# Attention over gathered neighbours: the transposes of later keys placed between the scores of the next duo and the values of the present one

## The chip, the cores and the metric

The kernel runs on one core of a Trainium2 chip. The metric is the device time of one execution in microseconds (us). The time before is the median of three runs; a measured difference of less than about 0.3% cannot be told from none.

## The reference

One layer of a graph network: a masked attention with eight heads over 4096 nodes, then a mixture of eight experts of which each node uses two.

```python
x = x + _L0_gnn_ref(_layernorm(x), adj, Wks, Wqs, Wvs, Wo)
x = x + _L0_ffn_ref(_layernorm(x)[None], Wg, bg, W1, b1, W2, b2)[0]

def _L0_gnn_ref(node_matrix, adjacency_matrix, Wks, Wqs, Wvs, Wo):
    adj = jnp.maximum(adjacency_matrix, eye)
    q, k, v = (einsum('nd,hdk->hnk', node_matrix, W) for W in (Wqs, Wks, Wvs))
    scores = einsum('hqk,hmk->hqm', q, k) * kd ** (-0.5)
    scores = scores + 0.01 * eye - 1e16 * (1.0 - adj)
    att = softmax(scores, axis=-1)
    return einsum('hqm,hmk,hko->qo', att, v, Wo)
```

N is 4096, the model width 512, the key width 64. The adjacency matrix is sparse, and its first rows and columns are denser than the last ones. In the expert part (`_L0_ffn_ref`), a gate of 8 columns picks two experts for each node, and their outputs are summed with softmax weights.

## The kernel before, in words

The program has four stages in one instruction stream. It is scheduled by hand (`tc.manual_schedule()`, L106): each engine runs its instructions in the order in which the Python code issues them. Engines are TensorE (PE), VectorE (DVE), ScalarE (ACT), GpSimd (POOL) and the DMA issuer SP.

1. Up to about 455 us: layer norm, projections to q, k and v, and lists of the neighbours that occur in each tile of 128 queries. Keys, values and mask words go to `kv_d` in DRAM, queries to `q_d`.
2. Up to about 1640 us: attention, the stage of the change.
3. A short stretch that works out which rows go to which expert (L1142 to L1198).
4. From about 1692 us: the experts.

In stage 2 each of the 32 query tiles is a list of steps (L644 to L655). A step treats 128 keys, or twice 128 keys for the two halves of the queries. There are three kinds: "own" (the tile's own rows), "both" (128 gathered keys for all 128 queries), and "split" (two gathers of 128 keys, each for 64 queries). `ROOM` (L31) says how many steps of each kind a tile has. All in all there are 32 own, 115 both and 123 split steps. Steps of one tile are taken two at a time, in the order of the list; such a pair, or a single last step, is a duo (L659 to L662). There are S = 144 duos.

A step passes through four functions:

- `gather` (L686): an indirect DMA on POOL's queue for each 128 keys (own rows come by SP) into a row of a ring of 24 rows (`RING`, L630). `issue` (L1070) asks for duos up to five ahead (`AHEAD`, L1062), as far as rows of the ring are free.
- `turn` (L716): PE transposes the keys, four transposes for 128 keys, into PSUM tile `pkT` (L723). ACT copies `pkT` to `kT` in SBUF (L725). DVE unpacks the mask bits to `t` (L735), and for own steps makes `m` (L742).
- `scores` (L749): PE multiplies `kT` by the queries into `ps` (L760): for a split step 64 matmuls on 64x64 pieces of the array, for the others 16 on 64x128 pieces. ACT takes the exponential into `pr` (L767). DVE applies the mask (L771 or L773).
- `values` (L779): PE multiplies `pr` by the values in the ring into the tile's accumulator `o` (L788), 32 matmuls on 128x64 pieces for a step.

Behind the last duo of a tile, `end_of` (L803) divides by the sums at once (`scale`) and puts jobs into later iterations: `flip_o` (transposes, L820) one later, `project` (L828) and `residual` (L837) two later. After every fourth tile, `route` (L855) puts in jobs that spread over some eight iterations: `norm` on ACT (L890), `flip` (transposes, L901), `gate` (L910), `rank` and `place` on DVE (L919 to L942), `number_places` (PE, tile `pp`, L947) with `keep_places` (DVE, L954), `pick` and `weigh` (DVE, then one exponential on ACT, L1011), `finish`, and `scatter` (POOL, L1029).

The order around the change is that of the main loop (L1117 to L1138). In iteration n it issues: scores of duo n+1, values of duo n, the loads of `issue`, the jobs of iteration n, and then the turn of duo n+3. Three duos are turned ahead of the loop (L1112 to L1115).

PSUM is a second order that matters. `ps_r` (L635) has three tiles of two banks each, and `bank` (L666) hands them out in rotation to everything in this stage but the accumulator `o`: `ps` and `pkT`, one tile for each step, and the tile of each PE job (`po`, `py`, `px`, `pl`, `pp`). So the tile handed out as number k is the buffer of number k-3, and a PE group that takes it must wait until ACT or DVE has emptied that one. The accumulator `o` has one buffer of two banks. In SBUF, `kT` and `pr` have four buffers, `t` six.

Of the kernel before, what the change touches and what calls it, by code (L numbers as in the profile page):

```python
# [70 lines left out]
def fast(tc, dram, flag, x, adj, Wks, Wqs, Wvs, Wo, Wg, bg, W1, b1, W2, b2, out):  # L71
    with ExitStack() as ctx:
        _fast(ctx, tc, dram, flag, x, adj, Wks, Wqs, Wvs, Wo, Wg, bg, W1, b1, W2, b2, out)


def _fast(ctx, tc, dram, flag, x, adj, Wks, Wqs, Wvs, Wo, Wg, bg, W1, b1, W2, b2, out):
# [248 lines left out]
    with ExitStack() as s1:  # L325
# [198 lines left out]
        def job(n, f, *args):  # L524
            jobs.setdefault(n, []).append(lambda: f(*args))
# [108 lines left out]
    with ExitStack() as s2:  # L634
# [76 lines left out]
        def load_xi(i):  # L711
            xs_[i] = mid.tile([P, W], F32, tag="x", bufs=10, name=f"x_{i}")
            queue = nc.sync if i < NT - 3 else nc.scalar
            queue.dma_start(out=xs_[i][:, :D], in_=x[ts(i, P), :])
# [355 lines left out]
        def issue(upto, n):  # L1070
            nonlocal issued, rows_
            while issued < min(upto, S):
                sts = [steps[s] for s in duos[issued]]
                need = sum(max(1, len(st["at"])) for st in sts)
                if any(behind[(rows_ + k) % RING] > n for k in range(need)):
                    return
                for s in duos[issued]:
                    st = steps[s]
                    if st["k"] == 0:
                        load_q(st["i"])  # L1080
                    st["to"] = []
                    for x in range(max(1, len(st["at"]))):
                        k = rows_ % RING
                        behind[k] = issued
                        rows_ += 1
                        st["to"].append(ring[:, k * KVW : (k + 1) * KVW])
                        gather(s, x)
                issued += 1
# [3 lines left out]
        def load_weights(n):  # L1092

            for k in range(PARTS):
                over_ = range(k * SW // KVW, min(RING, ((k + 1) * SW - 1) // KVW + 1))
                if issued == S and wparts[k] is None and all(behind[r] <= n for r in over_):
                    load_part(k, ring[:, k * SW : (k + 1) * SW].bitcast(F32))

        def load_part(k, t):
            v = t.rearrange("p (e f) -> p e f", e=E)  # L1100
            from_, c = (W1, k) if k < DC else (W2, k - DC)
            for e in range(E):
                nc.sync.dma_start(out=v[:, e], in_=from_[e, ts(c, P), :])
            wparts[k] = v

        def duo(f, n):
            if n < S:
                for s in duos[n]:
                    f(s)
# [6 lines left out]
        n = 0  # L1116
        while n < S or any(k >= n for k in later):  # L1117
            duo(scores, n + 1)
            duo(values, n)
            if n < S:  # L1120
                end = steps[duos[n][-1]]
                if end["last"]:
                    end_of(end["i"], n)
                    load_xi(end["i"])
                issue(n + 1 + AHEAD, n)
                load_weights(n)
            todo = later.pop(n, [])
            if n >= S:
                todo.sort(key=lambda job: -job[0])
            for _, job in todo:  # L1130
                job()
            duo(turn, n + 3)
            if n == S:
                s3.close()
                wff = ctx.enter_context(tc.tile_pool(name="wff", bufs=1))
                for k in range(PARTS, DC + HC):
                    load_part(k, wff.tile([P, SW], F32, name=f"w_{k}"))
            n += 1  # L1138
# [854 lines left out]
```

## Time and profile before

| What | Value |
|---|---|
| Median of 3 runs | 2074.48 us (2071.14 to 2076.76) |
| The profiled execution | 2230.39 us, its span 2228.6 us |
| PE busy in the span | 2003.9 us (90%), 25491 matmuls |
| DVE, ACT, POOL busy | 959.3, 790.9, 611.7 us |
| Attention stage (455 to 1640 us): PE busy | 1021.4 of 1185.0 us, at a granted clock of 0.93 |
| The same: DVE, ACT, POOL busy; DMA share | 534.8, 527.0, 464.9 us; 0.71 |
| Expert stage (1692 to 2228.6 us): PE busy | 517.7 of 536.6 us |

The profile is of one execution on the chip. A line of a group names a line of the kernel, the engine, the operation, the tile written and those read, the pieces of the array in use (64*64 means 64 rows by 64 columns of it), the shapes and a count; then busy time and mean duration, and the idle time of the engine ahead of these instructions with its causes. "issue" as a cause means that the engine waited for nothing that the profile shows. In a timeline, each line is a run of like instructions: start, duration from the first start to the last end, engine, line. Matmuls are pipelined, so that the end of one may lie after the start of the next. A wait for several semaphores is put down to the one that came last.

### The profile page before, as it was taken

Reading aid. Unit: us, or ns where it says so; the run is one execution under the profiler, and the core shown is the slowest. Engines: PE = TensorE matmul, PEld = TensorE weight load, DVE = VectorE, ACT = ScalarE, POOL = GpSimd, SP = SyncE. Lnnn points to the kernel's source line nnn. Section 1 sums busy time; section 2 is a strip of 40 time slices with the busy share of each in tenths; the row PEclk is TensorE's granted clock in tenths of the full one; section 3 lists DMA queues with packets and bytes.
Section 4 is the critical chain, followed back from the end, with each engine's and each line's share of the span. In section 5 each row is a group of like instructions: output and inputs, shape, how many; then the busy total and the mean of one; then the engine's idle time right before and its main releaser. Section 6 shows DMA issues by size and latency. Waiting matters only on the chain. (4 is left out here: it accounts for less than half of the span.)

```text
span 2228.6 us, 59742 instructions
## 1 busy us (share of the span) xinstructions
PE 2003.9 (90%) x25491; PEld 1329.7 (60%) x25491; DVE 959.3 (43%) x2501; ACT 790.9 (35%) x1152; POOL 611.7 (27%) x721
## 2 busy tenths in 40 slices
PE   9899999979999879888969697887967999999996
PEld 4344444459887757767858586776754444444443
DVE  3455655525444434534535344443554333333332
ACT  3232333235554534534535253443421222222221
POOL 2000000054444345433243443324122222222221
PEclk9999999989999979989989798998978999999998
DMA  9778775287777568767576575766686455565542
GB/s 371 253 251 257 255 246 179 77 350 252 246 259 257 201 228 266 249 206 239 190 267 232 202 255 204 255 201 222 227 278 195 104 115 113 111 144 111 110 72 44
DMA packets 193411, 462.01 MB, mean 207 GB/s; under 512 B 30384, under 2 KB 46768, under 8 KB 193008
## 3 DMA queue, kind: packets, MB, share of 16 engines
q0 software_dynamic: 67024, 249.44, 36.8%
q1 hardware_dynamic: 101808, 177.51, 24.8%
q10 hardware_dynamic: 24304, 31.11, 4.0%
q8 instruction: 206, 3.38, 0.6%
q14 instruction: 69, 0.57, 0.1%
HBM read 385.37 MB, written 72.64 MB: 206 GB/s over the span
## 5 line engine op out<-in xcount | busy, mean ns | idle before, releaser
L696 POOL DMA_INDIRECT ring<-kv_d,idx x361 | 407.3, 1128 | 978.1 <-ACT l L303 438.0
L760 PE MATMUL ps<-q,kT 64*64 64x64 f32 (+1 forms) x10224 | 356.5, 242 | 112.4 <-issue 96.0
L773 DVE SCALAR_TENSOR_TENSOR pr<-t,pr 128x1024 f32<-128x1024 uint16 x238 | 284.9, 1226 | 369.8 <-ACT pr L767 367.4
L760 PEld LDWEIGHTS ps<-q,kT 64*64 64x64 f32 (+1 forms) x10224 | 304.3, 151 | 166.1 <-issue 135.9
L788 PE MATMUL o<-ring,pr 128*64 128x65 f32 x8640 | 308.9, 228 | 31.6 <-issue 31.3
L725 ACT COPY kT<-pkT 128x512 f32<-128x512 f32 (+1 forms) x270 | 198.8, 783 | 375.5 <-PE pkT L723 268.6
L767 ACT ACTIVATE pr<-ps 128x1024 f32<-128x1024 f32 x270 | 271.4, 1025 | 139.4 <-PE ps L760 104.0
L788 PEld LDWEIGHTS o<-ring,pr 128*64 128x64 f32 x8640 | 282.1, 141 | 52.3 <-issue 37.5
L1341 PE MATMUL ph<-ring,xT 128*128 (+1 forms) x528 | 238.2, 594 | 0.8 <-ACT xT L1303 0.8
L723 PE MATMUL pkT<-ident,ring 128*128 128x128 f32 x1572 | 211.3, 282 | 18.3 <-issue 16.7
L723 PEld LDWEIGHTS pkT<-ident,ring 128*128 128x128 f32 x1572 | 180.0, 145 | 46.3 <-issue 38.7
L1392 POOL DMA_INDIRECT out_dram<-y,r x66 | 101.8, 1542 | 366.2 <-ACT y L1387 266.8
L1370 PE MATMUL py_e<-ring,hT 128*128 (+1 forms) x396 | 182.3, 596 | 1.6 <-ACT hT L1363 1.6
L1341 PEld LDWEIGHTS ph<-ring,xT 128*128 128x128 f32 (+1 forms) x528 | 91.3, 183 | 99.8 <-issue 98.7
L1387 ACT ACTIVATE y<-y,wt 128x512 f32<-128x512 f32 x66 | 47.6, 722 | 269.6 <-DVE y L1383 229.8
L604 PE MATMUL pv<-wv,xT 128*128 128x512 f32 x256 | 131.3, 608 | 0.0
L604 PE MATMUL pk<-wk,xT 128*128 128x512 f32 x256 | 130.4, 621 | 0.7 <-ACT xT L399 0.7
L589 PE MATMUL pq<-xT,wq 128*128 128x512 f32 x256 | 125.9, 607 | 0.0
L1029 POOL DMA_INDIRECT xs_d<-x,slot_i x64 | 64.6, 1010 | 203.2 <-DVE t L735 90.2
L828 PE MATMUL py<-wo,oT 128*128 128x512 f32 x256 | 119.3, 609 | 0.7 <-ACT oT L822 0.7
L1346 DVE COPY h<-ph 128x512 f32<-128x512 f32 x66 | 45.6, 692 | 169.6 <-PE ph L1341 166.1
L1370 PEld LDWEIGHTS py_e<-ring,hT 128*128 128x128 f32 (+1 forms) x396 | 67.2, 183 | 76.0 <-issue 74.1
(293 smaller groups left out, 1893.7 us busy)
## 6 DMA issues: line engine op xcount, KB each, us to landing
adj<-in_adj_dram SPq DMA_DIRECT2D x64, 1024.0 KB
wo<-in_L_ffn_W_dram SPq DMA_DIRECT2D x72, 256.0 KB
kv_d<-kvr ACTq DMA_DIRECT2D x32, 516.0 KB
ring<-kv_d SPq DMA_DIRECT2D x32, 516.0 KB
r<-xs_d SPq DMA_DIRECT2D x57, 258.0 KB
ring<-in_L_ffn_W_dram SPq DMA_DIRECT2D x56, 256.0 KB
xt<-in_x_dram SPq DMA_DIRECT2D x32, 256.0 KB
q_d<-qT ACTq DMA_DIRECT2D x32, 256.0 KB
```

Source lines behind the costliest of these rows:

```text
L589: nc.tensor.matmul(pq, w["q"][:, c, ts(p, P)], xTs[b][:, c, :], start=(c == 0), stop=(c == DC - 1),)
L604: nc.tensor.matmul(pk, xTs[b][:, c, ts(t, P)], w[n][:, c, :], start=(c == 0), stop=(c == DC - 1),)
L696: nc.gpsimd.indirect_dma_start(out=g, out_offset=None, in_=kv_d, in_offset=bass.IndirectOffsetOnAxis(ap=idx[i // GL][:, i % GL, a : a + 1] ...
L723: nc.tensor.transpose(pk[:, x * NP + p, :], g[:, ts(p, P)], ident)
L725: nc.scalar.copy(kT[:, : nk * NP], pk[:, : nk * NP])
L760: nc.tensor.matmul(ps[c : c + nk, r, p * P + x * nq : p * P + (x + 1) * nq], kT[r * KD : (r + 1) * KD, p, c : c + nk], q[r * KD : (r + 1) ...
L767: nc.scalar.activation(pr.rearrange("p h q -> p (h q)"), ps.rearrange("p r f -> p (r f)"), AF.Exp)
L773: nc.vector.scalar_tensor_tensor(pr, st["t"].unsqueeze(1).to_broadcast([P, H, P]), 0.0, pr, op0=ALU.is_gt, op1=ALU.mult,)
L788: nc.tensor.matmul(o[c * HALF : (c + 1) * HALF, h // NP, (h % NP) * VW : (h % NP + 1) * VW], pr[:, hd * NP + p, c * HALF : (c + 1) * HALF] ...
L828: nc.tensor.matmul(hold["py"], hold["oT"][:, c, :], wo[:, c, :], start=(c == 0), stop=(c == NP - 1),)
L1341: nc.tensor.matmul(ph[a], xTs[b][:, c, a], w, start=(c == 0), stop=(c == DC - 1), skip_group_check=b >= FULL,)
L1370: nc.tensor.matmul(py[a], hTs[b][:, c, a], w, start=(c == 0), stop=(c == HC - 1), skip_group_check=b >= FULL,)
```

## The change

One line moves. The turn of duo n+3 is issued directly behind the scores of duo n+1 and ahead of the values of duo n, and no longer at the end of the iteration behind the values, the loads and the jobs. The prologue, the count of instructions, the buffers and the loads are the same. For the last three duos there is nothing left to turn, so that 141 turns move.

```diff
         while n < S or any(k >= n for k in later):
             duo(scores, n + 1)
+            duo(turn, n + 3)
             duo(values, n)
             if n < S:
                 end = steps[duos[n][-1]]
...
             for _, job in todo:
                 job()
-            duo(turn, n + 3)
             if n == S:
                 s3.close()
```

`duo(f, n)` (L1106) calls f for each step of duo n. `turn` issues transposes on PE (L723), the copy on ACT (L725) and the mask's unpacking on DVE (L735, L742); it issues no DMA. On each of the three engines these instructions come ahead of the values' matmuls, the division of a tile's end and the jobs, where they came behind them.

## Prediction

> **What bounds the kernel now.** I read the page's busy times, then the table of stages, the waits of PE within the attention, and last the timeline around them.
>
> ```profile
> PE 2003.9 (90%) x25491; PEld 1329.7 (60%) x25491; DVE 959.3 (43%) x2501; ACT 790.9 (35%) x1152; POOL 611.7 (27%) x721
> ...
> PE ps L760 <- issue: 91.1, 123, 9.5
> PE o L788 <- issue: 28.2, 38, 2.9
> PE pkT L723 <- issue: 9.0, 13, 3.0
> PE ps L760 <- DVE place L954: 7.1, 5, 1.8
> ...
> PE ps L760 <- ACT oT L822: 2.9, 5, 1.8
> PE ps L760 <- ACT kT L725: 1.5, 3, 1.0
> PE pkT L723 <- ACT x2T L903: 1.2, 2, 0.9
> ```
>
> PE is busy for 90% of the span, the next engine for 43%. So the sum of PE's work sets the time, and this change adds no matmul. The waits (600 to 1640 us; total, times, longest) say what PE lacks in the attention: 128 us "issue", mostly in the middle of a run of matmuls, where no data can be late, and only 7.1 + 2.9 + 1.5 + 1.2 = 12.7 us for results of other engines. Those 12.7 us are all that a better order can win from other engines. A third cost is in the timeline of PE (start, duration, line, count):
>
> ```profile
> 562.01 0.66 PE L820 MATMUL po<-ident,on 128*128 128x128 f32 x4
> 562.51 1.47 PE L723 MATMUL pkT<-ident,ring 128*128 128x128 f32 x12
> 563.91 2.58 PE L760 MATMUL ps<-q,kT 64*64 64x64 f32 x80
> 566.42 2.09 PE L788 MATMUL o<-ring,pr 128*64 128x65 f32 x64
> 568.44 3.70 PE L828 MATMUL py<-wo,oT 128*128 128x512 f32 x8
> 571.98 1.47 PE L723 MATMUL pkT<-ident,ring 128*128 128x128 f32 x12
> ```
>
> Subtract each start from the end of the line above. A job (L820, L828) and a turn (L723), both on 128*128 pieces, overlap by 0.16 us (562.67 less 562.51; 572.14 less 571.98). Turn to scores, scores to values, values to job overlap by 0.07 us only. So whenever the piece of the array changes, 0.09 us of overlap is lost. And a turn of 12 behind a job takes 1.47 us, behind values 1.53 us:
>
> ```profile
> 1106.35 2.09 PE L788 MATMUL o<-ring,pr 128*64 128x65 f32 x64
> 1108.37 1.53 PE L723 MATMUL pkT<-ident,ring 128*128 128x128 f32 x12
> ```
>
> **What the Trainium skill says.** "TensorEngine Tiling (Array Packing)", section Key Properties: changing the tiling mode, not just the tile, drains the TensorE. The trace agrees, and prices it: 0.09 us of overlap, and 0.06 us for a slower first transpose. "TensorE: Matmul & The Clock Gate", section on the array's architecture: ScalarE and VectorE are strict FIFOs, and only weight loads are pulled ahead on PE. The trace agrees: `keep_places` (L954, below) runs only after the masks queued ahead of it. "Runtime: NRT & Kernel Launch", section Instruction fetch mechanics: instructions come by DMA in blocks of 256. The trace has 206 packets and 3.38 MB on such a queue, 16 KB each; that this is what "issue" in mid-run waits for, no run here shows.
>
> **The change, part by part.** Call the PE groups S (scores), T (turn), V (values), J (jobs). The order S V J T becomes S T V J.
>
> *Changes of the piece.* Without PE jobs a round is S V T before and S T V after: three changes in both, each with 0.07 us of overlap whichever pair it is, so nothing. With PE jobs J and T were neighbours on the same pieces: S V JT had three changes, S T V J has four. I went through the loop's job times (L848 to L860, L1040 to L1060) for each of the 141 iterations that turn something: 30 hold `flip_o`, 30 `project`, 12 more only flips, gates or `number_places`. That is 72 x (0.09 + 0.06) = +10.8 us, all on PE, beside nothing.
>
> *Waits that go.* The five for `place` look like this one:
>
> ```profile
> 1224.25 0.19 PE L947 MATMUL pp<-chosen,below 128*128 128x32 bf16 x1
> 1224.69 2.35 DVE L773 SCALAR_TENSOR_TENSOR pr<-t,pr 128x1024 f32<-128x1024 uint16 x2
> 1224.78 1.04 PE L723 MATMUL pkT<-ident,ring 128*128 128x128 f32 x8
> 1226.96 0.18 DVE L954 TENSOR_TENSOR place<-pp,start_e 128x32 f32<-128x32 f32 x1
> 1227.20 0.29 PE L760 MATMUL ps<-q,kT 64*64 64x64 f32 x4 [1.38 <-DVE place L954]
> ```
>
> `pp` is done at 1224.4, DVE empties it only behind two masks, at 1227.1, and the first score behind the turn needs that PSUM buffer. After the change the scores of one duo and, where `pp` is the iteration's only bank, that whole pair (2 us) pass before the buffer comes round: tile k waits for tile k-3, so behind S1 S2 T1 T2 J the next first turn waits for J. Two of the five are of this kind and vanish. Three have `pp` and `po` together; there the second score waits for `pp`. Its need comes 1.0 us later and DVE arrives 0.5 us later (the turn's unpacking, 0.56 us for three, L735, is now ahead of it), so 1.4 becomes about 0.45 us on my reckoning at each. Total 7.1 becomes 1.4: -5.7 us. The oT waits follow `weigh`, whose exponential holds ACT until DVE has done `pick` (2.2 us); the buffer's next user is again a turn, 2 us of scores later, but DVE starts 0.9 us later. 2.9 becomes 0.8: -2.1 us. The kT waits (second score behind the copy of the first turn) and the x2T waits go: -2.7 us.
>
> *Waits that come.* The second turn of a pair now takes the buffer of the first score, so it waits for that exponential in every iteration. Bounds from this place:
>
> ```profile
> 1215.51 2.06 PE L760 MATMUL ps<-q,kT 64*128 64x128 f32 x32
> 1216.72 1.95 ACT L767 ACTIVATE pr<-ps 128x1024 f32<-128x1024 f32 x2
> 1217.50 1.15 PE L788 MATMUL o<-ring,pr 128*64 128x65 f32 x32
> ```
>
> The first exponential (mean 1.025 us) ends at 1217.74. In the new order T1 would start at 1217.50 in place of V, and T2 after 4 transposes (0.11 each, plus 0.06) at 1218.0, after 8 at 1218.45. Margin 0.2 to 0.7 us if ACT is free when the score ends, and it is: its four operations of a duo (two of 1.0, two of 0.5 to 1.0) fit into S, T and V of 5 to 6 us. With jobs it is late in five iterations where two copies and two `norm`s (0.75 each) queue up: about 0.5 us each, +2.5 us. From below it cannot be a gain; from above see the first rival.
>
> *What is moved past what.* `turn` issues no DMA, so SP's and POOL's queues keep their order. Gathers wait for V of an earlier duo, which now comes one T later in its round, while T comes earlier by V and J, at most about 8 us in all. The gathers run far ahead: the last starts at 1584.7 and the last transpose at 1622.6, and the landing of the software queue's packets, 5.5 us in the middle and 7.0 at the ninth tenth from issue, leaves 25 us or more behind the first 15 duos and 14 us at the fourth, the first that moves. If that cover were gone, PE would stand for what is missing. On DVE, `scale` and the jobs now stand behind the unpacking (0.3 to 0.85 us); they need V, which ends one T later anyway. V waits for `pr` of the round before, and has T more time.
>
> *Sum.* 10.8 - 5.7 - 2.1 - 2.7 + 2.5 = +2.8 us. Against the profiled execution 2230.4 becomes 2233.2. The median of the timed runs is 155.9 us less, about the 128 us of "issue" with its slowed clock; that part is likely smaller there. The sum consists of PE time at full clock and of queues behind ACT and DVE, so I add it as it is: 2074.5 + 2.8 = 2077.3, within the 0.3% (6.2 us) that a measurement of this kernel tells from no change. The case's own range, from half the savings kept to all of them, is 2072 to 2083.
>
> **The rivals.** *The exponential in the way (slower).* The margin of T2 is 0.2 us at its smallest. If ACT starts the first exponential later than in the quoted place, each turn pays; it decides from 0.25 us of lateness on. At a mean of 0.1 us in 141 iterations that is +14: 2091. For it: the same buffer serves every round, and own and both steps have the small margin. Against it: 0.06 us from the end of the score to ACT's start in the quoted place. Half of it gives 2084.
> *Smoother supply (faster).* 91.1 + 28.2 us are lost in the middle of S and V, the runs dense in instructions. T and J between them spread the dense runs. If a tenth goes, -12: 2065. Against it: S and V were neighbours before, and V and S are so in half of the new rounds; and the timed runs have less of this idle time.
> *Turning was never the limit.* If the waits stay and the drains too, 2085; if the drains hide in the starved stretches and nothing else moves, 2074.
> *Keys late.* With 25 us of lead, 2% at most.
>
> **How the numbers follow.** The forecast 0.45 (a quarter of it above 2081), exponential or kept waits 0.30, smoother supply 0.20, others 0.05. Faster by over 0.3%: 0.21; within: 0.38; slower: 0.41. The range reaches into both rivals: 2066 to 2089.
>
> **What would show it.** Right: PE's L723 lines of 8 or 12 at about the 1.53 us form in every round; L788 to a job and a job to L760 with 0.07 us of overlap; the wait for `place` at 2 us or less; PE's busy time up by some 5 to 11 us. Wrong: a wait of L723 for `pr` L767 of over 5 us in total (the first rival); "issue" at L760 and L788 well below 119 us, with a faster median (the second); any wait of L723 for DMA.

## The result, and the profile after

The changed kernel takes 2064.1 us (median of 6 runs, 2060.94 to 2068.36); the kernel before, run beside it, 2075.11 us (6 runs, 2071.14 to 2076.76). The ratio is 0.9955, 95% interval 0.9939 to 0.9971: faster by 6.0 to 12.7 us, where the forecast was +2.8 us. The profiled execution took 2068.36 us, its span is 2066.5 us.

One thing is needed to read the numbers below: whole executions of the kernel before take either about 2075 us, as in this comparison, or about 2222 us, as in its profile and in all the experiments, so the two traces differ by more than the change, and the kernel before has no trace at 2075 us.

From the page of the changed kernel: the engines' busy time, and the granted clock in 40 slices.

```profile
PE 1942.0 (94%) x25491; PEld 1283.8 (62%) x25491; DVE 959.3 (46%) x2501; ACT 785.1 (38%) x1152; POOL 571.1 (28%) x721
...
PEclk9999999999999999999999999999979999999998
```

The count of matmuls is the same, and PE is even more clearly the bound. What PE waited for in the changed kernel, 600 to 1480 us, since its attention ends some 158 us earlier than in the trace of before (total, times, longest):

```profile
PE o L788 <- issue: 22.6, 20, 2.6
PE ps L760 <- issue: 19.1, 16, 3.7
PE pkT L723 <- DMA ring<-kv_d: 6.0, 2, 5.6
PE o L788 <- DVE t L735: 2.6, 1, 2.6
PE ps L760 <- ACT x2T L903: 0.9, 3, 0.3
PE ps L760 <- DVE place L954: 0.8, 2, 0.4
PE py L828 <- issue: 0.6, 1, 0.6
PE pkT L723 <- ACT oT L822: 0.5, 1, 0.5
```

The waits for `place`, `oT` and `kT` are down to 0.8, 0.5 and nothing. There is no wait of a turn (L723) for an exponential (`pr`, L767). "issue" is 42 us where it was 128 (in 600 to 1640 us), but that difference belongs to the two executions: in a later one of the changed kernel (2291 us, below) it is 104 us. New is a wait for keys, 6.0 us. The 2.6 us at the values are put down to DVE's unpacking, which had ended 1 us before; they are of the kind of the "issue" gaps (see the table of two kinds of gap). The timeline of PE in the changed kernel (start, duration, line, count):

```profile
759.28 2.06 PE L760 MATMUL ps<-q,kT 64*128 64x128 f32 x32
761.27 1.53 PE L723 MATMUL pkT<-ident,ring 128*128 128x128 f32 x12
762.73 2.09 PE L788 MATMUL o<-ring,pr 128*64 128x65 f32 x64
764.75 2.25 PE L760 MATMUL ps<-q,kT 64*64 64x64 f32 x80
766.93 1.97 PE L723 MATMUL pkT<-ident,ring 128*128 128x128 f32 x16
768.83 2.09 PE L788 MATMUL o<-ring,pr 128*64 128x65 f32 x64
770.85 0.66 PE L820 MATMUL po<-ident,on 128*128 128x128 f32 x4
771.43 0.75 PE L760 MATMUL ps<-q,kT 64*64 64x64 f32 x36
```

The order is S T V, then J where there is one, and the overlap is 0.07 us at most of the changes (759.28 + 2.06 less 761.27; 768.83 + 2.09 less 770.85): the job is now among values and scores, with a change of piece on both sides, as the prediction had it. The turn of 12 takes 1.53 us, as priced. Everything outside the attention takes what it took: the experts 529 us in both traces, the work ahead of the attention 465 to 467 us. From the first transpose to the last value matmul it is 1177.8 us in the trace of before and 1021.6 us here.

### The profile page after: what moved, and what is told of

Its sections match the earlier page's. It is cut to its first block, busy times and chain, and to the rows that moved or that the text cites. A ratio compares the mean times of both kernels' runs of the same rounds, so it can differ in the third digit from the quotient of the medians.

```text
span 2066.5 us, 59701 instructions
## 1 busy us (share of the span) xinstructions
PE 1942.0 (94%) x25491; PEld 1283.8 (62%) x25491; DVE 959.3 (46%) x2501; ACT 785.1 (38%) x1152; POOL 571.1 (28%) x721
## 5 line engine op out<-in xcount | busy, mean ns | idle before, releaser
L696 POOL DMA_INDIRECT ring<-kv_d,idx x361 | 360.9, 1000 | 873.7 <-ACT l L303 437.1
L767 ACT ACTIVATE pr<-ps 128x1024 f32<-128x1024 f32 x270 | 270.4, 1025 | 376.1 <-PE ps L760 373.9
L760 PE MATMUL ps<-q,kT 64*64 64x64 f32 (+1 forms) x10224 | 308.5, 237 | 26.4 <-issue 24.4
L788 PE MATMUL o<-ring,pr 128*64 128x65 f32 x8640 | 297.3, 226 | 26.9 <-issue 24.0
L760 PEld LDWEIGHTS ps<-q,kT 64*64 64x64 f32 (+1 forms) x10224 | 274.8, 149 | 69.5 <-issue 56.4
L788 PEld LDWEIGHTS o<-ring,pr 128*64 128x64 f32 x8640 | 273.9, 140 | 54.6 <-issue 49.4
L723 PE MATMUL pkT<-ident,ring 128*128 128x128 f32 x1572 | 206.0, 280 | 12.7 <-DMA ring<-kv_d 6.0
L725 ACT COPY kT<-pkT 128x512 f32<-128x512 f32 (+1 forms) x270 | 198.5, 787 | 15.0 <-DMA q_d<-qT 6.7
L723 PEld LDWEIGHTS pkT<-ident,ring 128*128 128x128 f32 x1572 | 171.0, 142 | 29.8 <-issue 7.7
L1029 POOL DMA_INDIRECT xs_d<-x,slot_i x64 | 70.2, 1097 | 186.6 <-DVE x L1025 159.3
L1370 PEld LDWEIGHTS py_e<-ring,hT 128*128 128x128 f32 (+1 forms) x396 | 67.2, 183 | 75.9 <-issue 74.1
```

What stands on the lines that cost most here:

```text
L696: nc.gpsimd.indirect_dma_start(out=g, out_offset=None, in_=kv_d, in_offset=bass.IndirectOffsetOnAxis(ap=idx[i // GL][:, i % GL, a : a + 1] ...
L723: nc.tensor.transpose(pk[:, x * NP + p, :], g[:, ts(p, P)], ident)
L725: nc.scalar.copy(kT[:, : nk * NP], pk[:, : nk * NP])
L760: nc.tensor.matmul(ps[c : c + nk, r, p * P + x * nq : p * P + (x + 1) * nq], kT[r * KD : (r + 1) * KD, p, c : c + nk], q[r * KD : (r + 1) ...
L767: nc.scalar.activation(pr.rearrange("p h q -> p (h q)"), ps.rearrange("p r f -> p (r f)"), AF.Exp)
L788: nc.tensor.matmul(o[c * HALF : (c + 1) * HALF, h // NP, (h % NP) * VW : (h % NP + 1) * VW], pr[:, hd * NP + p, c * HALF : (c + 1) * HALF] ...
```

## The experiments

Two theories. **Supply**: PE lacks instructions in its densest runs, the scores (on the 64*64 pieces a weight load and a matmul every 14.8 ns; values take 30 ns for such a pair, transposes 109 ns), and the order and the gathers' traffic decide how much; the waits and drains of the prediction cancel. **Waits and drains**: the time is what these terms make it, and the supply is the same in every order. Ratios are to the kernel before on the same chip, with 95% intervals; code is shown as an edit of the kernel before where nothing else is said, with cuts marked by dots.

**Unchanged kernel, again.** No edit.

> The kernel before, unchanged, for a second profile. Both theories: 2071 to 2077 us. Theory 'waits' (the gain of the change is the buffer waits of scores for place, oT and kT that fall away, less four changes of the array's piece in place of three): the attention shows 15 to 25 us of PE waits for DVE and ACT, and about as much issue idle in the middle of L760 and L788 as the changed kernel has (50 us). Theory 'supply' (the gain is a smoother supply of instructions): issue idle in the middle of L760 and L788 is 12 us or more above the changed kernel's 50 us, and the waits for DVE and ACT are 10 us or less.

Measured: 2218.41 us, ratio 0.9987 (0.9968 to 1.0006), before 2221.85. The kernel does not differ from itself, as it must be, but the 2071 to 2077 us that both theories had expected were missed.

**Turn directly behind the values (S V T J).**

```diff
             duo(values, n)
+            duo(turn, n + 3)
...
-            duo(turn, n + 3)
```

> Order scores, values, turn, jobs: the turn is ahead of the jobs but still behind the values. PSUM buffers go round as in the changed kernel, but turn and jobs are neighbours on the same piece of the array, so that a round has three changes of piece again. Theory 'waits': the same waits fall away as in the changed kernel and 72 x 0.15 = 10.8 us of drains are not added: ratio to before 0.990 (2054 us), 0.986 to 0.993. Theory 'supply': scores and values are neighbours again in every round as before, so the gain is lost: ratio 0.998 to 1.001 (2071 to 2077 us).

Measured: 2215.87 us, 0.997 (0.9956 to 0.9984), before 2221.85: between the two forecasts. A second time:

> Scores, values, turn, jobs once more, beside the changed kernel. Theory 'waits': 10 us below the changed kernel. Theory 'supply': above it, ratio to before 0.997 as in the first such run.

Measured: 2210.66 us, 0.9955 (0.9938 to 0.9972), before 2220.82. Jobs and turn stay neighbours, so no drain is added; it gains 0.3 to 0.45%. The second forecast failed in both theories, as the changed kernel, run beside it, was 82 us slower.

**Turn and jobs both ahead of the values (S T J V).** The jobs' block moves with the turn.

```diff
             duo(scores, n + 1)
+            duo(turn, n + 3)
+            todo = later.pop(n, [])
...
+            for _, job in todo:
+                job()
             duo(values, n)
```

> Order scores, turn, jobs, values: the turn is where the change puts it, but the jobs come ahead of the values. PSUM buffers go round as in the changed kernel; turn and jobs are neighbours on the same piece, three changes a round. Theory 'waits': ratio 0.990 (2054 us), as without the extra drains. Theory 'supply': turn still parts scores from values, but values and the next scores are always neighbours: ratio 0.995 to 1.000 (2064 to 2075 us), not below the changed kernel's 2064.

Measured: 2403.76 us, 1.0826 (1.0796 to 1.0857): 182 us slower with the same matmuls, and far outside both forecasts (0.990, and 0.995 to 1.000). The largest wait in the whole trace of this kernel:

```profile
PE ps L760 <- issue: 135.1, 319, 1.7
```

The scores stand directly behind the values in every round and stop in mid-run 319 times. In the 104 such rounds that I compared, from 600 us on and away from the stretches in which DMAs of POOL scatter rows, the scores take 157 us more than their matmuls' own 14.8 or 57.5 ns each.

**The changed kernel on these chips.** No further edit.

> The changed kernel, unchanged, beside the kernel before on one chip. Theory 'waits' (buffer waits for place, oT and kT fall away, 10.8 us of drains come): the same 8 to 11 us less wherever it runs, ratio 0.995 to 0.997, and the waits of PE for DVE and ACT fall by some 20 us. Theory 'supply' (PE starves less in the middle of scores and values): the gain grows with the idle time that PE has there: 9 us where the kernel before takes 2075 us, 15 us or more where it takes 2222 us (ratio 0.993 or less).

Measured: 2292.41 us, 1.0324 (1.0291 to 1.0357), before 2220.82. **The sign turns over**: 71.6 us slower here, 9 us faster in the comparison of the result; both theories had expected a gain. So beside it one execution of the kernel before:

> The kernel before, for a profile from the same chip as the changed kernel. Theory 'waits': waits of PE for DVE and ACT in the attention 20 us above the changed kernel's. Theory 'supply': the issue idle in the middle of L760 and L788 is 15 us or more above it, the waits for DVE and ACT by 13 us at most.

Measured: 2226.15 us. The attention takes 1176.9 us in it and 1238.5 us in the changed kernel; all else is alike. In the timeline of the changed kernel of this job:

```profile
690.51 2.09 PE L788 MATMUL o<-ring,pr 128*64 128x65 f32 x64
692.53 0.50 PE L760 MATMUL ps<-q,kT 64*64 64x64 f32 x17
693.24 0.33 PE L760 MATMUL ps<-q,kT 64*64 64x64 f32 x4 [0.21 <-issue]
693.98 0.36 PE L760 MATMUL ps<-q,kT 64*64 64x64 f32 x5 [0.41 <-issue]
694.70 0.66 PE L760 MATMUL ps<-q,kT 64*64 64x64 f32 x26 [0.36 <-issue]
695.60 0.36 PE L760 MATMUL ps<-q,kT 64*64 64x64 f32 x6 [0.25 <-issue]
```

The 64 values take the 2.09 us that they take elsewhere; the scores behind them stop after 17 matmuls and then again and again, which is no wait for data, as one copy brought the keys of the whole step. The waits of the same kernel, 600 to 1480 us:

```profile
PE ps L760 <- issue: 78.4, 166, 2.3
PE o L788 <- issue: 14.1, 16, 1.8
PE pkT L723 <- issue: 11.6, 17, 1.8
PE pkT L723 <- ACT pr L767: 8.6, 9, 2.8
PE ps L760 <- DVE place L954: 0.8, 2, 0.4
```

And of the kernel before, in the execution of 2226 us, same stretch:

```profile
PE ps L760 <- issue: 83.2, 116, 9.6
PE o L788 <- issue: 16.1, 22, 2.9
PE pkT L723 <- issue: 8.4, 12, 2.7
PE ps L760 <- DVE place L954: 5.7, 4, 1.8
```

`place` goes from 5.7 to 0.8 as foretold, and the first rival's wait (a turn for an exponential) exists here with 8.6 us: too small for 70. The "issue" lines are hardly different (so neither forecast for this pair came true), because the gaps between single matmuls that are too short to be listed count as busy time. So I took, for each run of scores, the time from its first to its last start, less its count by the nominal distance (14.8 or 57.5 ns). By what stands ahead of it, from 600 us on, without the stretches with scatters:

| Kernel | ahead of the scores | rounds | mean excess, us | sum, us |
|---|---|---|---|---|
| before (2226) | turn | 108 | 0.48 | 51.5 |
| changed (2291) | values | 44 | 1.58 | 69.6 |
| changed (2291) | jobs | 66 | 0.52 | 34.1 |
| S V T J (2215) | turn | 44 | 0.79 | 34.8 |
| S V T J (2215) | jobs | 65 | 0.23 | 15.1 |
| S T J V (2384) | values | 104 | 1.51 | 157.2 |
| changed (2068) | values | 33 | 0.16 | - |

Scores behind transposes or jobs lose 0.2 to 0.8 us, behind values 1.5 us. In the execution of 2068 us they lose 0.16 behind values. From the first transpose to the last value matmul the scores take 49 us more in the changed kernel (2291) than in the kernel before (2226), the turns 15 more, the jobs 5 more and the values 8 less.

**Turn and scores alternating (S1 T1 S2 T2 V).**

```diff
-            duo(scores, n + 1)
+            for k in range(2):
+                for f, m in ((scores, n + 1), (turn, n + 3)):
+                    for s in (duos[m] if m < S else [])[k : k + 1]:
+                        f(s)
...
-            duo(turn, n + 3)
```

> Score, turn, score, turn, values: the finest mixture of scores and turns. Two more changes of piece in each round that has two steps on both sides (about 118 of 144), at about 0.29 us for the pair with its slower first transpose: +34 us on PE. Theory 'waits': slower than the changed kernel by that, ratio to before 1.011 (1.008 to 1.015). Theory 'supply': the dense scores are parted once more, so that a part or all of it comes back: ratio 0.990 to 1.003.

Measured: 2262.47 us, 1.0205 (1.0169 to 1.0241): 30 us below the changed kernel, although it has two more changes of piece in a round. By waits and drains alone it had to be slower. Both ranges were missed, though: they had been set for a changed kernel near 1.00, not 1.0324.

**One step's turn on each side of the values (S T1 V T2 J).**

```diff
             duo(scores, n + 1)
+            for s in (duos[n + 3] if n + 3 < S else [])[:1]:
+                turn(s)
             duo(values, n)
+            for s in (duos[n + 3] if n + 3 < S else [])[1:]:
+                turn(s)
...
-            duo(turn, n + 3)
```

> From the changed kernel: the first step's turn stays between scores and values, the second step's goes behind the values, ahead of the jobs. No dense run (scores, values) stands directly behind another. Theory 'supply, by what stands ahead' (scores that start directly behind values starve for instructions: in the profile of e4 1.58 us a round too long, 0.52 behind jobs; in that of e5 0.48 behind turns): where the kernel before takes 2222 us, about 60 us come back from e4's 2292 and about 10 go for one more change of piece in the rounds without PE jobs: 2225 to 2245, ratio 1.002 to 1.010. Where it takes 2075 us, scores behind values lose only 0.16 us in the changed kernel's profile, so nothing comes back: 2064 to 2075. Theory 'waits and drains alone': 10 us slower than the changed kernel at either place (ratio 1.037 or 1.000).

Measured: 2234.97 us, 1.0069 (1.0049 to 1.009), before 2220.12. As foretold by the supply theory. In rounds without PE jobs it has a drain more than the changed kernel, and it is 57 us below it: half a turn between values and scores is most of the cure.

**Useless transposes in the gap.** The changed kernel, with eight transposes of the identity (44 us of PE in all, by estimate) between values and scores in the 37 rounds without any job.

```diff
+            if not todo and n + 3 < S:
+                idle = bank(f"idle_{n}", [8, P])
+                for k in range(8):
+                    nc.tensor.transpose(idle[:, k, :], ident, ident)
```

> From the changed kernel: in the 37 rounds without any job, eight transposes of the identity (useless work) stand between values and the next scores: 8 x 0.11 us and one more entry and exit of their piece of the array, 0.3 us, so 37 x 1.2 = 44 us more of PE work. Theory 'supply, by what stands ahead': where the kernel before takes 2222 us they cost about nothing, since scores behind sparse work lose 1.06 us less a round: ratio 1.025 to 1.037 beside 1.032 of e4; where it takes 2075 us they cost 35 to 44 us: ratio 1.013 to 1.017. Theory 'waits and drains alone': +44 us at either place (1.052 or 1.017).

Measured: 2298.8 us, 1.0344 (1.0317 to 1.037), where the changed kernel had 1.0324 (1.0291 to 1.0357): the added PE work costs nothing that can be told from 0. In the two traces the added transposes take 38 us; the scores take 17 us less in return and the turns 11 less. So much of the time was there to be filled, though most of the cost of scores behind values stays.

**Without the gathers.** Once the 24 rows of the ring are filled, no more rows are gathered; each tile's own rows are loaded whole in their place. The attention so works on stale keys and the routing differs (the experts take 556 us); the instructions of PE are the same.

```diff
-                    out=g[:, :HV], in_=kv_d[1 + i * P : 1 + (i + 1) * P, :HV]
+                    out=g, in_=kv_d[1 + i * P : 1 + (i + 1) * P, :]
...
-                nc.gpsimd.indirect_dma_start(
...
+                if rows_ <= RING:
+                    nc.gpsimd.indirect_dma_start(
```

Order before, changed order, S V T J:

> The kernel before with the gathers left out once each of the 24 ring rows has been filled; later steps use old keys and masks, and own rows are loaded whole (580 KB in place of 516). PE, ACT and DVE do the same work. If the traffic of the gathers is what slows PE's supply of instructions: issue idle in the middle of scores and values falls from 120 us to 40 us or less and the time to 2070 to 2120 us (the 26 us stretches at the scatters may stay). If it isn't: 2200 to 2225 us.

> The changed kernel with the same gathers left out; to be compared with e10. If supply stays slow: 2270 us or more, 1.03 times e10, as with gathers. If supply is free, theory 'waits are larger than the first profile showed' (buffer waits of PE above 20 us where it isn't held up otherwise, drains 10.8 us): 9 to 12 us below e10. Theory of the prediction's sum (waits of 12.7 us): e10 plus 0 to 5 us.

> Scores, values, turn, jobs, with the same gathers left out. If supply is free and the waits are what is gained: 10 us below e11, as it has no extra drains. If only the place of turn between scores and values gains: as e10.

Measured: 2083.17, 2082.98 and 2083.0 us, each 0.9375 (at most 0.9353 to 0.9396), before 2222.32. The attention is 1005.2, 1002.9 and 1006.4 us, where it was 1177 with the gathers. The changed order is neither 70 us slower nor the 9 to 12 us faster that one theory had expected. Waits with the order before, 600 to 1480 us (lines one higher than in the kernel):

```profile
PE ps L761 <- issue: 17.1, 26, 1.5
PE o L789 <- issue: 11.1, 24, 1.1
PE ps L761 <- DVE place L955: 4.4, 4, 1.4
...
PE ps L761 <- ACT oT L823: 3.7, 6, 1.9
PE ps L761 <- ACT kT L726: 2.2, 3, 1.3
```

With the changed order:

```profile
PE ps L761 <- issue: 24.3, 41, 1.2
PE o L789 <- issue: 7.5, 12, 1.1
...
PE ps L761 <- ACT x2T L904: 0.9, 3, 0.3
PE ps L761 <- DVE place L955: 0.8, 2, 0.4
PE pkT L724 <- ACT pr L768: 0.8, 3, 0.3
```

4.4 + 3.7 + 2.2 = 10.3 us of waits become 2.5: -7.8 us, and -8.4 us (12.6 to 4.2) with the smaller ones for other engines. The drains, by the busy time of PE in 455 to 1640 us (first number behind the length; order before, then changed order):

```profile
455.00:1640.00 1185.00, 1107.40 (x21710) 904.83 (x21709) 594.88 (x1517) 557.90 (x697) 116.86 (x202) 0.96 0.30 96
```

```profile
455.00:1640.00 1185.00, 1116.82 (x21718) 903.02 (x21717) 598.82 (x1522) 554.68 (x699) 120.58 (x203) 0.96 0.30 97
```

+9.4 us, but some 2 us of it are work of the experts, which start 2.1 us earlier. From the first transpose to the last value matmul the same 21166 matmuls keep PE busy for 953.4 and 960.5 us: +7.1 us. -8.4 and +7.1 leave -1.3 us; the attention is 2.3 us shorter and the times differ by -0.2, each from runs that spread over 6 us. For S V T J I had expected -10, as it has no added drain; that fell. Its waits do not go away:

```profile
PE ps L761 <- DVE place L955: 4.5, 4, 1.4
PE ps L761 <- ACT kT L726: 2.1, 8, 0.3
```

The PSUM tiles go round as in the changed order; what differs is that no values stand between a turn and the next scores. That this is why the waits stay was not tested.

**Every second gather.** The condition becomes the following, else as above; again stale keys.

```diff
+                if rows_ <= RING or rows_ % 2:
```

> The kernel before with about half of the gathers left out after the ring's first filling (every second row keeps its old content; own rows loaded whole). Theory 'supply under gather traffic': between 2083 and 2222 us, about 2085 to 2120, with an issue idle of 30 to 60 us in the middle of scores and values. If it doesn't come from traffic but from the gathers' mere presence: near 2200.

> The changed kernel with the same half of the gathers left out; to be compared with e13. Theory 'the sign goes with the loss to supply': at this light load 3 to 10 us below e13 (ratio 0.995 to 0.999), as beside 2075 us. If scores behind values starve at any load: 5 to 40 us above e13.

> Scores, values, turn, jobs with the same half of the gathers left out. It was 0.996 of before with all gathers and 1.000 with none, so 0.996 to 1.000 of e13 by either theory; if turn between scores and values is what gains at a light load, e14 lies below it.

Measured: 2115.74 us, 0.9492 (0.9467 to 0.9518); 2140.29 us, 0.9609 (0.9579 to 0.9638); 2116.41 us, 0.949 (0.9463 to 0.9517); before 2231.81. I had hoped that a lighter load would turn the sign to that of the comparison of the result. It does not: the changed order is 24.6 us slower, and S V T J is at the level of the order before (0.7 us more). What the scores lack, order before and changed order in turn (600 to 1480 us):

```profile
PE ps L761 <- issue: 43.0, 71, 2.8
PE o L789 <- issue: 17.6, 25, 2.5
```

```profile
PE ps L761 <- issue: 52.0, 117, 1.7
PE o L789 <- issue: 7.6, 12, 1.2
```

So the price of the changed order is 0, about 25 and about 70 us with no, half and all gathers. The wait of the scores grows and that of the values shrinks: the shortage moves to the run that now stands behind another dense one. With the gathers the traffic went, and also POOL's work on them and their writes into SBUF; these were not parted.

**Two kinds of gap in mid-run.** The "issue" gaps of over 0.15 us within a run of like matmuls are of two kinds. In the execution of 2068 us all 44 are *long*: they last 0.2 to 3.7 us, each ends at instruction 193 or 194 of a block of 256, counted over PE's instructions in the trace, and 1.2 to 1.6 us after a packet on PE's instruction queue has landed (206 packets of 16 KB bring its some 52000 instructions, so about 256 each). For example, the 64 values of this round stop once:

```profile
755.42 1.21 PE L788 MATMUL o<-ring,pr 128*64 128x65 f32 x33
758.20 1.15 PE L788 MATMUL o<-ring,pr 128*64 128x65 f32 x31 [1.57 <-issue]
```

In every other trace most gaps are *short*: their median is 0.4 us, they often follow each other at 0.72 us or twice that, and they come at any place of a block and with no fixed distance to a packet, as in the lines at 693 to 696 us above. Counts and sums in the attention:

| Order (execution, us) | long | sum, us | short | sum, us |
|---|---|---|---|---|
| before (2226) | 18 | 22.4 | 173 | 105.5 |
| changed (2291) | 8 | 8.9 | 250 | 121.2 |
| S V T J (2215) | 15 | 18.2 | 185 | 103.7 |
| S T J V (2384) | 6 | 7.8 | 355 | 157.3 |
| S T1 V T2 J (2232) | 8 | 10.3 | 222 | 112.0 |
| before, half of the gathers | 16 | 16.5 | 107 | 63.4 |
| changed, half | 5 | 6.2 | 147 | 67.2 |
| S V T J, half | 18 | 18.0 | 107 | 56.6 |
| before, no gathers | 8 | 5.2 | 56 | 28.2 |
| changed, no gathers | 3 | 1.9 | 54 | 36.5 |
| S V T J, no gathers | 6 | 4.8 | 59 | 34.2 |
| changed (2068) | 44 | 49.0 | 0 | 0 |

The change makes the long gaps fewer in all three pairs, by 13.5, 10.3 and 3.3 us, as does every order with a turn between scores and values; and it makes the short ones longer in sum, by 15.7, 3.8 and 8.3 us. The execution of 2068 us has only the kind that the change makes fewer.

Taking out the scatters alone was not tried, since a later stage uses what they write as indices.

## Why the prediction was wrong, step by step

*Changes of the piece (+10.8 us).* Right in kind, somewhat too large: 0.07 us of overlap at the new changes, and PE's busy time in the attention up by 7.1 us without gathers.

*Waits that go (-5.7, -2.1, -2.7).* Right in total: 7.8 to 8.4 us go net without gathers, 8.0 were foretold with the +2.5 below. In the execution of 2068 us `place` is left with 0.8 (1.4 foretold), `oT` with 0.5 (0.8), `kT` with none; `x2T` stays with 0.9, which I had at zero.

*Waits that come (+2.5).* Too large: none in the execution of 2068 us, 0.8 us for the turns without gathers. The first rival (each turn late for the exponential, +14) did not come; in the execution of 2291 us it shows 8.6 us.

*What is moved past what.* "25 us or more" of lead for the keys, and so 2% for "Keys late", was read from an execution whose PE stood still more often. In the execution of 2068 us PE is faster and the lead, from the landing of a gather's packets to the first transpose of its duo, shrinks to 2.3 us at its smallest behind the first 15 duos. For rows that are not gathered it fails once by 5.6 us (and once by 0.4). The changed kernel's timeline:

```profile
1281.44 2.12 PE L760 MATMUL ps<-q,kT 64*64 64x64 f32 x67 [0.17 <-issue]
1289.16 1.94 PE L723 MATMUL pkT<-ident,ring 128*128 128x128 f32 x8 [5.60 <-DMA ring<-kv_d]
1291.03 3.08 PE L788 MATMUL o<-ring,pr 128*64 128x65 f32 x64
```

The late rows are a tile's own, which SP loads. Whether the kernel before has this wait at 2075 us, no trace tells.

*Smoother supply: the step that failed.* The sum was added "as it is", and so the change of "issue", PE's gaps in mid-run, was put at nothing. Against the rival it was said that S and V were neighbours before, and V and S are so in half of the new rounds. That counts neighbours and not their order, nor what feeds the densest run. The runs showed in its place that these gaps depend on the order: with the same matmuls the time moves from 0.9955 to 1.0826 of the kernel before, and the changed order costs 0, 25 or 70 us with no, half and all gathers. This term is larger than all the others together. In the comparison of the result the measured change is -9.3 us (0.9955 of 2075.11). Waits and drains are +2.8 us by the forecast and -1.3 us as measured without gathers, so that some -8 to -12 us are left, near the -12 us of the rival, 2065 us, which I had given a chance of 0.20. The range ended at 2066, 1.9 us above the measured time: it left out the lower half of that rival. Two of my own signs of being wrong are there: a wait of L723 for a DMA (6.0 us), and "issue" at L760 and L788 well below 119 us (41.7 us) with a faster median, though most of this second difference lies between the two executions.

**What is shown and what is not.** Shown: without gathers, waits and drains cancel to within 2 us; PE's gaps in mid-run depend on what stands ahead of the scores and on the gathers; the long gaps are waits for a packet of instructions, and the change makes them fewer in each of three pairs. Only argued: that the gain of 9 us at 2075 us is that, since the kernel before has no trace there. What speaks for it is that the execution of 2068 us has long gaps alone, and that its scores lose just 0.16 us behind values, so that the penalty of 2222 us is absent. Not shown: that the short gaps are a lack of instructions too. That the traffic holds PE up in another way would fit them as well, and no run parts the two. Open: what makes the short gaps, and why the execution of 2068 us has none. The number of gathers alone does not decide the sign, since at half of them the changed order was still slower. S V T J was the best at 2222 us (0.9955 and 0.997 of before); no run of it is at 2075 us.

## What to carry to other kernels

When a saturated engine's idle time lies mostly in the middle of its densest runs of instructions, the order of dense and sparse runs can be the largest term (here 0.9955 to 1.0826 of the time), and "unchanged" is no estimate of it: look at what stands ahead of the densest run. Take the cause of the traffic out (here the gathers) in both orders: what is then left of the difference is mostly the part that waits and drains account for. And read leads and idle times from a profile whose own time is that of the timed runs: here the profiled execution, 7% above the median, had another kind of gap and 25 us of lead where there were 2.3.

## What the runs showed of the hardware

- PE can lack instructions. "Runtime: NRT & Kernel Launch", section Instruction fetch mechanics, has the crossing of a 16 KiB block mostly hidden. Here it is not: in the execution of 2068 us, 49.0 us of PE's attention are 44 gaps of 0.2 to 3.7 us in mid-run, each at the same place of a block of 256 instructions (193 or 194 in the trace's count) and ending 1.2 to 1.6 us behind the landing of a packet.
- A second kind of gap, 0.4 us in the median and often at distances of 0.72 us, comes at any place of a block: 173 gaps and 105.5 us in the kernel before (2226 us), none in the execution of 2068 us. Elsewhere it is least without gathers (28 to 37 us); more than half of that is while POOL issues scatters (L1029), which is 5% of the attention. The attention falls from 1177 to 1005 us when the gathers go.
- In executions of 2222 us the instruction queue moves no packet for 15 to 28 us at each group of scatters: 25.5 us at 787.8, 26.5 at 1111.1, 28.2 at 1242.2 in the trace of before. The longest such stretch in the attention of the execution of 2068 us is 11.4 us.
- The clock goes along. "TensorE: Matmul & The Clock Gate", section on the clock gate, sets it by how busy PE has been. The time at half clock in the attention was 151.8 us in the kernel before (2226 us), 222.7 in the changed one (2291 us), 44.4 in the execution of 2068 us and 61 to 75 without gathers. So a gap can cost twice: behind the 5.6 us wait above the granted clock was 0.50 up to 1293.2 us, and 64 value matmuls took 3.08 us in place of 2.09.
- Entering 128*128 pieces behind others costs 0.09 us of overlap and makes the first transpose 0.33 in place of 0.27 us.
